# Attention scores in three pairs of PSUM banks, one bank shared by the sums from squares and the projections, and lists of chosen tokens spread by TensorE

## The chip, the cores and the metric

The kernel runs on one core of a Trainium2 chip. The metric is the device time of one execution in microseconds (us). The engines are called as the profile calls them: PE (TensorE, matrix products), PEld (its weight loads), DVE (VectorE), ACT (ScalarE), POOL (GpSimd) and SP (SyncE, which issues most of the DMAs); SPq is SP's instruction queue. PE writes its results to PSUM, which has eight banks of 2 KB a partition; a bank holds 512 float32 numbers a partition.

## The reference, cut to what matters

The program is a chain of four layers on 8 images of 56 x 56 tokens (S = 3136) with 128 channels: a deformable convolution, a whitening of the channels, an attention layer with a mixture of experts (L2), and a linear attention with a second mixture of experts (L3). The change touches the last two.

```python
# L2: attention with keys = queries = values, 8 heads of 16
h = (_ln(t) @ W_k.T).reshape(B, S, 8, 16).transpose(0, 2, 1, 3)
attn = softmax(einsum('bhqd,bhkd->bhqk', h, h) / 4)
t = t + (einsum('bhqk,bhkd->bhqd', attn, h) as tokens) @ W_o.T
# both FFNs: every one of 64 experts takes its best 8 tokens of an image
probs = softmax(_ln(t) @ gate_w.T + gate_b, axis=1)          # over the tokens
topv, topi = top_k(probs over the tokens, 8)                 # [B, 8, 64]
pooled = einsum('bked,bke->bed', _ln(t) gathered at topi, topv)
out = expert_e(pooled)          # two layers, 128 -> 512 -> 128, own weights for each e
t = t + zeros.at[topi].add(out * topv)                       # scattered back
```

The scores are symmetric, since keys and queries are the same: exp(score) of block (b, a) is the transpose of that of block (a, b).

## The kernel before

**Attention (`attend`).** The 3136 tokens of an image are cut into 25 tiles of 128 (`KT`) and 8 query blocks (`NQ`) of three tiles (384 tokens, `KB` = 3); the last block has 448. The work goes through 16 units, one for each image and group of four heads. In a unit each block b, from the last to the first, is multiplied with its own tiles and with those of about half of the other blocks (`stage`): 25 steps for the last block, 13 for each of the others, 116 a unit, 1856 in all. One step is one key tile against one query block, for four heads:

- `scores` (L1168): four matmuls on PE, one for each head on its 32 rows, into four PSUM banks; then ACT takes the exponential, heads 0 and 1 in one instruction over the two banks of the tile `p_s2` (L1175), heads 2 and 3 singly (L1177, tiles `p_s`).
- `weigh` (L1220): `av` collects exp x values over the steps of a block, in one bank.
- `transpose_squares` (L1186), where the tile lies off the block's diagonal: DVE transposes the exponentials in 32 x 32 squares into `sq`, two instructions a step.
- After three such steps (one tile block) `move_squares` has SP issue twelve DMAs (L1202) that put the 32-row squares in their places in `x`, and POOL copies the four on the diagonal (L1213, two a step). This is a job; there are 448.
- `from_squares`: at least `AGE` = 5 steps after its job was made, `avx` (L1220) weighs `x` for the mirrored block, in three steps of a job, into one bank; after the third `take` adds it to the block's sum `acc` on DVE (L1239).

So 1344 steps have a part of an `avx`, 512 have none. The order of the instructions on every engine is the order in which this loop writes them (`manual_schedule`, L1094). On PE a step is: the scores of the next step, a piece of `finish` if there is one, `av`, `avx`.

**`finish` and `choose`.** When the five contributions of a block are in, the generator `finish` divides and, for the second head group of an image, projects, adds the residual, normalises and computes the gate's logits `pr`. It is cut by `yield` into pieces, and the loop does one piece in every second step (`i % 2`); its matmuls (`p_av`, `p_tr`, `p_o`, `p_tr`, `p_g`) use a bank of their own, pool `psm`. When all eight blocks of an image are there, `choose` (L1567 and on) finds the eight best tokens for each expert on DVE (`best`, `at`), their softmax weights (ACT, `every`), writes tokens and weights `found` [64 experts, 2, 8] to DRAM (`route`, L1596, SP) and reads them back as `rw` [128, 2, 4] (`load_choices`, L1628, SP), one chosen token in each partition and column; four gathers by POOL (L1633) and a matmul with the expert pattern (`p_pool`, L1619) make `pooled`.

PSUM in this stage: `ps2` one tile of two banks, `pss` three of one, `psa` (`av`), `psx` (`avx`) and `psm` (pieces) one each: eight banks.

**After the attention.** `run_experts` runs the 64 experts in 16 groups of four, four groups' weights loaded ahead on SP's queue (L1734, L1737); between groups it advances `Spread.prepare` of the images, which reads each list again (`rw`, and `every`, the 512 tokens on all partitions, L1657), gathers the chosen tokens and builds a 512 x 512 matrix that adds up the weights of tokens chosen by several experts (L1674 on DVE, L1678 on POOL). `Spread.run` scatters the result (L1702). Then come the sums of the linear attention's context, `linear_layer` with `choose` once an image, and `run_experts` again for L3.

Of the kernel before, what the change touches and what calls it, by code (L numbers as in the profile page):

```python
# [46 lines left out]
TOP = 8  # L47
# [1021 lines left out]
def attend(tc, k, w, low, tok, kT_in, va_in, t_out, gate_w, gate_b, routes, pooled):  # L1069
# [11 lines left out]
    with ExitStack() as ctx:  # L1081
# [5 lines left out]
        xp = ctx.enter_context(tc.tile_pool(name="atx", bufs=3))  # L1087
        pss = ctx.enter_context(tc.tile_pool(name="ats", bufs=3, space=PSUM))
        ps2 = ctx.enter_context(tc.tile_pool(name="at2", bufs=1, space=PSUM))
        psa = ctx.enter_context(tc.tile_pool(name="ata", bufs=1, space=PSUM))  # L1090
        psx = ctx.enter_context(tc.tile_pool(name="atp", bufs=1, space=PSUM))
# [67 lines left out]
        def scores(u, b, a, i, m):  # L1159

            kT, q, width = keys[u, a][0], queries[u, b], blocks[b][1]
            e = ep.tile([128, 4, QB + 64], F32, name="e")
            s2 = ps2.tile([128, 2, 512], F32, name="p_s2")
            ss = [s2[:, 0], s2[:, 1]]
            ss += [pss.tile([128, 512], F32, tag="s", name="p_s") for _ in range(2)]
            for j in range(4):
                rows = slice(32 * j, 32 * j + 32)
                nc.tensor.matmul(  # L1168
                    ss[j][:m, :width],
                    kT[rows, 128 * i : 128 * i + m],  # L1170
                    q[rows, :width],
                    start=True,
                    stop=True,
                )
            nc.scalar.activation(e[:m, :2, :width], s2[:m, :, :width], AF.Exp)  # L1175
            for j in (2, 3):
                nc.scalar.activation(e[:m, j, :width], ss[j][:m, :width], AF.Exp)  # L1177
            exps[u, b, a, i] = e
# [43 lines left out]
        def from_squares():  # L1222
            u, b, a, x, i, _ = jobs[0]
            assert not (i == 0 and len(jobs) == 1 and moves)
            if i == 0:
                sums[0] = psx.tile([128, QB], F32, tag="x", name="avx")
            e = [x[:, :, (KB * j + i) * 32 : (KB * j + i) * 32 + 32] for j in range(4)]
            weigh(sums[0], u, b, i, 128, e, i == 0, i == KB - 1)
            jobs[0][4] += 1
            if i == KB - 1:  # L1230
                jobs.pop(0)
                take(u, a, sums[0])

        def take(u, b, av):

            width = blocks[b][1]
            to = by_square(acc[b])
            if done[b]:
                nc.vector.tensor_tensor(to, to, in_order(av), ALU.add)  # L1239
            else:  # L1240
                nc.vector.tensor_copy(to, in_order(av))
                if width > QB:
                    nc.vector.tensor_copy(acc[b][:, QB:], av[:, QB:width])
            done[b] += 1
            if done[b] == (1 if b == last else 5):
                work = finish(*parts[u], b)
                urgent.append(work)
                later.append(work)

        def finish(n, g, b):  # L1250

# [22 lines left out]
            yield  # L1274
            if g == 0:
                return
            yield
# [12 lines left out]
            yield  # L1290
# [20 lines left out]
            yield  # L1311
            yield
# [10 lines left out]
            yield  # L1323
# [5 lines left out]
            yield  # L1329
# [5 lines left out]
            yield  # L1335
            ready.append(n)
            if ready.count(n) == NQ:
                yield from choose(nc, k, wp, psm, pr, t_out[n], routes[n], pooled[:, n])
# [21 lines left out]
        av = None  # L1360
        for i, (u, b, a, c, m) in enumerate(steps):
            if i + 1 < len(steps):
                scores(*steps[i + 1])
            if a < NQ and a != b:
                transpose_squares(u, b, a, c)
            keep_squares()
            if i % 2 and urgent:
                work = urgent.pop(0)
                if next(work, later) is later:
                    later.remove(work)  # L1370
            elif i % 2:
                advance(later)
# [29 lines left out]
        while urgent:  # L1402
            work = urgent.pop(0)
            if next(work, later) is later:
                later.remove(work)
        while later:
            advance(later)


def attend_any(tc, k, w, yv, kT_in, va_in, t_out, gate_w, gate_b, routes, pooled, t_g):  # L1410
# [26 lines left out]
    with ExitStack() as ctx:  # L1437
# [3 lines left out]
        for n in range(n_b):  # L1441
# [11 lines left out]
            for _ in choose(nc, k, wp, ps, pr, t_out[n], routes[n], pooled[:, n]):  # L1453
                pass
# [109 lines left out]
def choose(nc, k, wp, ps, pr, t_in, route, pooled):  # L1564
# [30 lines left out]
    with nc.allow_non_contiguous_dma(reason="512 choices"):  # L1595
        nc.sync.dma_start(route.rearrange("x j e -> e x j"), found)  # L1596
    rw = load_choices(nc, wp, route)
    for _ in range(4):
        yield
    rows = wp.tile([128, NC], I32, name="rows")  # L1600
    nc.vector.tensor_copy(rows, rw[:, 0])
# [11 lines left out]
    yield  # L1613
    nc.vector.tensor_tensor(rs, rs, rw[:, 1], ALU.mult)
# [6 lines left out]


def load_choices(nc, pool, route):


    rw = pool.tile([128, 2, NC], F32, name="rw")
    with nc.allow_non_contiguous_dma(reason="512 choices"):
        nc.sync.dma_start(rw, route.rearrange("x (c j) e -> (j e) x c", j=TOP // NC))  # L1628
    return rw
# [11 lines left out]
class Spread:  # L1641
# [3 lines left out]
    def __init__(self, tc, pool, n_b):  # L1645
# [3 lines left out]
        self.rows = pool.tile([128, n_b, NC], I32, name="s_r")  # L1649

    def prepare(self, tc, n, wp, route, t_in, first):
# [3 lines left out]
        rw = load_choices(nc, wp, route)  # L1655
        every = wp.tile([128, TOP * E], F32, name="every")
        nc.sync.dma_start(  # L1657
            every, route[0].rearrange("j e -> (j e)").partition_broadcast(128)
        )
        yield  # L1660
        rows = wp.tile([128, NC], I32, name="rows")
        nc.vector.tensor_copy(rows, rw[:, 0])
        for c in range(NC):
            gather(nc, self.x[:, n, c], t_in, rows[:, c : c + 1])
        if first:
            nc.vector.tensor_scalar(rw[:, 0], rw[:, 0], float(first), None, ALU.add)
        nc.vector.tensor_copy(self.rows[:, n], rw[:, 0])
        if first:
            nc.vector.tensor_scalar(rw[:, 0], rw[:, 0], -float(first), None, ALU.add)
        for c in range(NC):  # L1670
            out = self.weights[:, n]
            if c:
                out = wp.tile([128, TOP * E], F32, name="same")
            nc.vector.tensor_scalar(  # L1674
                out, every, rw[:, 0, c : c + 1], rw[:, 1, c : c + 1], ALU.is_equal, ALU.mult
# [298 lines left out]
def linear_layer(tc, k, w, low, cw, t_in, xT_in, t_out, out, gate_w, gate_b, routes, pooled):  # L1974
# [5 lines left out]
    with ExitStack() as ctx:  # L1980
# [5 lines left out]
        def group(n, g):  # L1986
# [72 lines left out]
            if g == NG - 1:  # L2059
                yield from choose(nc, k, wp, ps, pr, t_out[n], routes[n], pooled[:, n])  # L2060
# [30 lines left out]
def token_layers(tc, k, a, y, out):  # L2091
# [3 lines left out]
    with ExitStack() as ctx:  # L2095
# [9 lines left out]
        routes = [  # L2105
            [dp.tile([2, TOP, E], F32, name=f"route{i}_{n}") for n in range(n_b)]
            for i in range(2)
        ]
# [32 lines left out]
        dest = (t_a, *gates[0], routes[0], pooled[0])  # L2141
# [5 lines left out]
        with tc.tile_pool(name="ex2", bufs=AHEAD) as xp:  # L2147
            ex = Experts(tc, xp, a["L2_ffn_weight1"], a["L2_ffn_weight2"], AHEAD)
            run_experts(tc, k, ex, pooled[0], oe_d[0], routes[0], t_a, [0] * n_b, t_a)
# [4 lines left out]
        with tc.tile_pool(name="ex3", bufs=AHEAD) as xp:  # L2154
            ex = Experts(tc, xp, a["L3_ffn_weight1"], a["L3_ffn_weight2"], AHEAD)
            cw = context_weights(tc, k, w, mp, tot, den)
            dest = (cw, t_a, xT_d, t_c, out, *gates[1], routes[1], pooled[1])
# [3 lines left out]
            with both.Else():  # L2161
# [4 lines left out]
                tc, k, ex, pooled[1], oe_d[1], routes[1], t_c, firsts, [flat] * n_b  # L2166
# [3 lines left out]
def run_experts(tc, k, ex, pooled, oe, routes, t_in, firsts, dests):  # L2170


    with ExitStack() as ctx:
# [3 lines left out]
        todo = [  # L2177
            spread.prepare(tc, n, wp, routes[n], t_in[n], firsts[n])
            for n in range(len(t_in))
        ]  # L2180
        for _ in ex.run(k, pooled, oe):
            advance(todo, 2)
        while todo:
            advance(todo, 2)
# [57 lines left out]
```

## Time and profile before

| | us |
|---|---|
| median of 3 runs | 8446.42 |
| the runs | 8442.32 to 8447.27 |
| profiled execution | 8463.81 |
| its span, first to last instruction | 8462.0 |
| convolution and whitening, keys | 0 to 2388 |
| attention loop and what is left over after it | 2388 to 7310 |
| L2 experts and scatter | 7310 to 7490 |
| sums of the context | 7490 to 7741 |
| linear layer | 7741 to 8215 |
| L3 experts | 8215 to 8372 |
| last scatter | 8372 to 8462 |

In a timeline a line gives the start and the time from the first start to the last end of equal neighbouring instructions, then engine, source line, operation, output and inputs, shapes, and in brackets how long the engine had idled before and what ended that. A line of waits gives engine, line and what it waited for, then total, number and the longest. Matmuls overlap, so the distance of starts says more than their durations.

### The profile page before, as it was taken

How to read it: one execution, taken by the hardware profiler on the slowest of the kernel's cores; microseconds unless marked ns; L12 is line 12 of the kernel's file. 1: busy time of each engine (PE TensorE's matmuls, PEld its weight loads, DVE VectorE, ACT ScalarE, POOL GpSimd, SP SyncE). 2: the span in 40 equal slices, each digit the busy share in tenths (PEclk: the TensorE clock that was granted, in tenths of full speed). 3: DMA queues.
4: the chain of work that ended last, by engine and by line, in shares of the span. 5: the costliest groups of instructions: out<-in, count | busy, mean ns of one | idle time of the engine just before them, and what ended most of it. 6: DMA issues, size and time to landing. Idle time of an engine off the chain costs nothing. (4 is left out here: it accounts for less than half of the span.)

```text
span 8462.0 us, 158965 instructions
## 1 busy us (share of the span) xinstructions
PE 6881.1 (81%) x59199; PEld 2885.4 (34%) x59199; DVE 5195.3 (61%) x10405; ACT 4446.5 (53%) x8821; POOL 3375.8 (40%) x2891
## 2 busy tenths in 40 slices
PE   8976777755589998998999989989989999456734
PEld 4544444423323332332332323323323323135522
DVE  4457667515656676676666766766766766346751
ACT  2324555531256666666666666666666666046740
POOL 0003454541234444444444444444444444333653
PEclk6657777777789999999999999999999999589767
DMA  4333323236768777877777877877877777443544
GB/s 99 86 80 65 75 54 77 51 74 190 222 179 194 180 190 175 192 184 177 188 173 186 192 168 186 193 171 180 195 170 183 188 177 175 149 138 108 129 110 141
DMA packets 773029, 1278.98 MB, mean 151 GB/s; under 512 B 160341, under 2 KB 531498, under 8 KB 765226
## 3 DMA queue, kind: packets, MB, share of 16 engines
q1 hardware_dynamic: 762266, 1252.28, 60.9%
q0 software_dynamic: 6144, 12.60, 0.5%
q8 instruction: 478, 7.83, 0.4%
q10 hardware_dynamic: 3824, 3.68, 0.1%
q14 instruction: 317, 2.60, 0.1%
HBM read 290.36 MB, written 185.03 MB: 56 GB/s over the span
## 5 line engine op out<-in xcount | busy, mean ns | idle before, releaser
L1213 POOL COPY x<-sq 32x1152 f32<-32x1152 f32 x1792 | 2048.0, 1143 | 2320.7 <-issue 1164.7
L1186 DVE STREAM_TRANSPOSE sq<-e 128x768 f32<-128x768 f32 x2688 | 2446.7, 952 | 780.2 <-ACT e L1175 337.0
L1175 ACT ACTIVATE e<-p_s 128x768 f32<-128x768 f32 (+2 forms) x1856 | 1546.6, 833 | 1741.4 <-PE p_s L1168 1647.4
L1168 PE MATMUL p_s<-q,kT 32*128 32x384 f32 (+2 forms) x14848 | 1946.9, 550 | 101.4 <-DVE q L1154 27.0
L1220 PE MATMUL av<-e,va 128*32 128x384 f32 (+2 forms) x14848 | 1648.4, 516 | 14.3 <-DVE acc L1239 14.3
L1177 ACT ACTIVATE e<-p_s 128x384 f32<-128x384 f32 (+2 forms) x3712 | 1650.4, 501 | 0.1
L1220 PE MATMUL avx<-x,va 128*32 128x384 f32 x10752 | 1144.1, 498 | 169.8 <-DMA x<-sq 112.5
L1168 PEld LDWEIGHTS p_s<-q,kT 32*128 32x128 f32 (+1 forms) x14848 | 693.5, 181 | 1365.8 <-ACT e L1177 793.4
L1220 PEld LDWEIGHTS av<-e,va 128*32 128x32 f32 (+1 forms) x14848 | 293.4, 108 | 970.1 <-issue 896.5
L1220 PEld LDWEIGHTS avx<-x,va 128*32 128x32 f32 x10752 | 335.4, 111 | 791.7 <-issue 751.9
L1239 DVE TENSOR_TENSOR acc<-acc,avx 128x384 f32<-128x384 f32 x336 | 186.3, 554 | 342.5 <-PE avx L1220 341.3
L554 PE MATMUL p_f<-x1T,w 128*128 128x448 f32 x448 | 229.9, 634 | 99.9 <-ACT y L510 47.1
L116 PE MATMUL p_tr<-ident,xn 112*128 112x112 f32 x672 | 134.3, 339 | 189.3 <-DVE xn L107 145.6
L507 POOL TENSOR_TENSOR rs<-rs,mhalf 112x4 f32<-112x4 f32 x112 | 120.3, 1074 | 379.8 <-DVE rs L506 359.0
L504 DVE BATCH_NORM_STATS2 st<-p_tok 112x6 f32<-112x128 f32 x448 | 116.4, 277 | 250.8 <-PE p_tok L536 250.6
L1055 POOL TENSOR_TENSOR rs<-rs,mhalf 112x4 f32<-112x4 f32 (+2 forms) x136 | 168.5, 1239 | 253.2 <-DVE ntop L1853 126.8
L424 PE MATMUL p_w<-ident,wide 112*88 112x112 f32 x896 | 179.6, 362 | 105.3 <-ACT wT L426 38.5
L559 PE MATMUL p_f<-hid,w 128*128 128x448 f32 x448 | 213.9, 624 | 42.2 <-ACT hid L555 27.3
L366 POOL MEMSET wide<- 112x10416 f32 x1 | 8.8, 8779 | 584.6 <-DMA om_d<-om 584.6
L264 DVE SCALAR_TENSOR_TENSOR acc<-xp,dw,acc 128x3136 f32<-128x3136 f32 x64 | 223.0, 3485 | 2.3
L1901 ACT ACTIVATE xn<-t,ms,rs 112x128 f32<-112x128 f32 x448 | 185.3, 488 | 74.3 <-DVE ms L1894 74.3
L1308 POOL TENSOR_TENSOR rs<-rs,mhalf 128x3 f32<-128x3 f32 (+1 forms) x72 | 58.9, 820 | 400.8 <-DVE rs L1307 394.2
(337 smaller groups left out, 8562.4 us busy)
## 6 DMA issues: line engine op xcount, KB each, us to landing
x<-sq SPq DMA_DIRECT2D x5376, 144.0 KB
w<-in_L_ffn_weight_dram SPq DMA_DIRECT2D x64, 1024.0 KB
px<-strips SPq DMA_DIRECT2D x64, 616.0 KB
va_d<-va SPq DMA_DIRECT2D x16, 1600.0 KB
kT_d<-kT SPq DMA_DIRECT2D x16, 1568.0 KB
t<-t_a SPq DMA_DIRECT2D x16, 1568.0 KB
kT<-kT_d SPq DMA_DIRECT2D x112, 192.0 KB
va<-va_d SPq DMA_DIRECT2D x112, 192.0 KB
```

Source lines behind the costliest of these rows:

```text
L264: nc.vector.scalar_tensor_tensor(acc, view, dw[:, j : j + 1], acc, ALU.mult, ALU.add)
L424: nc.tensor.transpose(p[:, g], around[:, :, g], k.ident[:T, :T])
L554: nc.tensor.matmul(p, q.w1[:, f * 128 : (f + 1) * 128], x1T, start=True, stop=True)
L559: nc.tensor.matmul(p, q.w2[:, f], hid[:, f], start=(f == 0), stop=(f == 3))
L1168: nc.tensor.matmul(ss[j][:m, :width], kT[rows, 128 * i : 128 * i + m], q[rows, :width], start=True, stop=True,)
L1175: nc.scalar.activation(e[:m, :2, :width], s2[:m, :, :width], AF.Exp)
L1177: nc.scalar.activation(e[:m, j, :width], ss[j][:m, :width], AF.Exp)
L1186: nc.vector.transpose(sq[:, :, i, j : j + 2].rearrange("p s j c -> p j s c"), exps[u, b, a, i][:, j : j + 2, :QB].rearrange("p j (s c) -> ...
L1213: nc.gpsimd.tensor_copy(*moves.pop(0))
L1220: nc.tensor.matmul(out, keys[u, b][1][:m, i, j, :], e[j], start=start, stop=stop)
L1239: nc.vector.tensor_tensor(to, to, in_order(av), ALU.add)
L1901: nc.scalar.activation(out[:, i], x[:, i], AF.Identity, bias=ms[:, i : i + 1], scale=rs[:, i : i + 1])
```

## The change

Three things change.

1. In `attend` the scores go to `pss`, three tiles of two banks (six banks), so that each step has two tiles and two exponentials over two banks each. `ps2` and `psx` are gone; `avx` takes the one bank of `psm` that the pieces of `finish` and `choose` use.
2. A piece says by its `yield` whether the next one needs that bank (`True`). A piece that needs it only goes on when no job is part way (`free`), and `later` pieces at most every second step (`turn`).
3. The lists stay in SBUF, in `choices` [128, image, 2, 4]. `choose` spreads `found` over 128 partitions with two matmuls by the identity (`p_take`) in place of the write and read through DRAM. `Spread.prepare` no longer reads lists: it multiplies the identity by the tokens (`own`) and adds up over the partitions with a matmul by ones, which puts all 512 tokens on every partition (`every`, in PSUM).

```diff
@@ attend
         pss = ctx.enter_context(tc.tile_pool(name="ats", bufs=3, space=PSUM))
-        ps2 = ctx.enter_context(tc.tile_pool(name="at2", bufs=1, space=PSUM))
         psa = ctx.enter_context(tc.tile_pool(name="ata", bufs=1, space=PSUM))
-        psx = ctx.enter_context(tc.tile_pool(name="atp", bufs=1, space=PSUM))
         psm = ctx.enter_context(tc.tile_pool(name="atm", bufs=1, space=PSUM))
@@ scores
-            s2 = ps2.tile([128, 2, 512], F32, name="p_s2")
-            ss = [s2[:, 0], s2[:, 1]]
-            ss += [pss.tile([128, 512], F32, tag="s", name="p_s") for _ in range(2)]
+            ss = [pss.tile([128, 2, 512], F32, name="p_s") for _ in range(2)]
...
-            nc.scalar.activation(e[:m, :2, :width], s2[:m, :, :width], AF.Exp)
-            for j in (2, 3):
-                nc.scalar.activation(e[:m, j, :width], ss[j][:m, :width], AF.Exp)
+            for j in range(2):
+                nc.scalar.activation(
+                    e[:m, 2 * j : 2 * j + 2, :width], ss[j][:m, :, :width], AF.Exp
+                )
@@ from_squares
-                sums[0] = psx.tile([128, QB], F32, tag="x", name="avx")
+                sums[0] = psm.tile([128, QB], F32, tag="m", name="avx")
@@ finish: each yield now says whether the next piece needs psm
-            yield
+            yield False   # or True
@@ attend, the loop
+        def go_on(work):
+            try:
+                work[1] = next(work[0])
+            except StopIteration:
+                later.remove(work)
...
-            if i % 2 and urgent:
-                work = urgent.pop(0)
-                if next(work, later) is later:
-                    later.remove(work)
-            elif i % 2:
-                advance(later)
+            free = not jobs or jobs[0][4] == 0
+            if urgent and free:
+                go_on(urgent.pop(0))
+            elif later and i > turn + 1 and (free or not later[0][1]):
+                go_on(later[0])
+                turn = i
@@ choose
-        nc.sync.dma_start(route.rearrange("x j e -> e x j"), found)
-    rw = load_choices(nc, wp, route)
-    for _ in range(4):
-        yield
+    yield True
+    p = ps.tile([128, 2, NC], F32, tag="m", name="p_take")
+    for j in range(TOP // NC):
+        nc.tensor.matmul(
+            p[E * j : E * j + E],
+            k.ident[:E, :E],
+            found[:, :, j :: TOP // NC],
+            start=True,
+            stop=True,
+        )
     rows = wp.tile([128, NC], I32, name="rows")
-    nc.vector.tensor_copy(rows, rw[:, 0])
+    nc.vector.tensor_copy(rows, p[:, 0])
+    nc.vector.tensor_copy(taken, p)
@@ Spread.prepare
-        rw = load_choices(nc, wp, route)
-        every = wp.tile([128, TOP * E], F32, name="every")
-        nc.sync.dma_start(
-            every, route[0].rearrange("j e -> (j e)").partition_broadcast(128)
-        )
-        yield
         rows = wp.tile([128, NC], I32, name="rows")
-        nc.vector.tensor_copy(rows, rw[:, 0])
+        nc.vector.tensor_copy(rows, taken[:, 0])
         for c in range(NC):
             gather(nc, self.x[:, n, c], t_in, rows[:, c : c + 1])
...
+        own = wp.tile([128, NC, 128], F32, name="own")
+        nc.vector.tensor_tensor(
+            own,
+            k.ident.unsqueeze(1).to_broadcast([128, NC, 128]),
+            taken[:, 0].unsqueeze(2).to_broadcast([128, NC, 128]),
+            ALU.mult,
+        )
+        yield
+        every = ps.tile([128, TOP * E], F32, name="every")
+        nc.tensor.matmul(
+            every, self.ones, own.rearrange("p c q -> p (c q)"), start=True, stop=True
+        )
```

More of the change, by code (lines that the diff above doesn't have):

```diff
@@ L1066, in query_blocks, with attend @@
     ]
-def attend(tc, k, w, low, tok, kT_in, va_in, t_out, gate_w, gate_b, routes, pooled):
+def attend(tc, k, w, low, tok, kT_in, va_in, t_out, gate_w, gate_b, taken, pooled):
     nc = tc.nc
@@ L1168, in scores @@
                 nc.tensor.matmul(
-                    ss[j][:m, :width],
+                    ss[j // 2][:m, j % 2, :width],
                     kT[rows, 128 * i : 128 * i + m],
@@ L1245, in take @@
             if done[b] == (1 if b == last else 5):
-                work = finish(*parts[u], b)
+                work = [finish(*parts[u], b), True]
                 urgent.append(work)
@@ L1289, in finish @@
             nc.vector.tensor_copy(aT[:, :width], p[:, :width])
-            yield
+            yield True
             p = psm.tile([128, KB + 1, C], F32, tag="m", name="p_o")
@@ L1310, in finish @@
                 )
-            yield
-            yield
+            yield False
+            yield False
             xn = wp.tile([128, KB + 1, C], F32, name="xn")
@@ L1322, in finish @@
                 )
-            yield
+            yield True
             xT = wp.tile([C, QB + 64], F32, name="xT")
@@ L1328, in finish @@
             nc.vector.tensor_copy(xT[:, :width], p[:, :width])
-            yield
+            yield True
             p = psm.tile([E, 512], F32, tag="m", name="p_g")
@@ L1334, in finish @@
             )
-            yield
+            yield False
             ready.append(n)
             if ready.count(n) == NQ:
-                yield from choose(nc, k, wp, psm, pr, t_out[n], routes[n], pooled[:, n])
+                yield from choose(nc, k, wp, psm, pr, t_out[n], taken[:, n], pooled[:, n])
+        def go_on(work):
[3 more added lines that the diff above has]
+                later.remove(work)
         ready = []
@@ L1359, in attend @@
         scores(*steps[0])
-        av = None
+        av, turn = None, -2
         for i, (u, b, a, c, m) in enumerate(steps):
@@ L1401, in attend, with attend_any @@
             from_squares()
[L1402 to L1405, printed above, removed]
+        for work in urgent:
+            go_on(work)
         while later:
-            advance(later)
-def attend_any(tc, k, w, yv, kT_in, va_in, t_out, gate_w, gate_b, routes, pooled, t_g):
+            go_on(later[0])
+def attend_any(tc, k, w, yv, kT_in, va_in, t_out, gate_w, gate_b, taken, pooled, t_g):
     nc = tc.nc
@@ L1452, in attend_any @@
                 nc.vector.tensor_scalar(pr[:, cols], p, gate_b, None, ALU.add)
-            for _ in choose(nc, k, wp, ps, pr, t_out[n], routes[n], pooled[:, n]):
+            for _ in choose(nc, k, wp, ps, pr, t_out[n], taken[:, n], pooled[:, n]):
                 pass
@@ L1561, in attention_any, with choose @@
             divide(nc, k, wp, psm, av_sb, att, g, c)
-def choose(nc, k, wp, ps, pr, t_in, route, pooled):
+def choose(nc, k, wp, ps, pr, t_in, taken, pooled):
     best = wp.tile([E, TOP], F32, name="best")
@@ L1594, in choose @@
     nc.vector.tensor_scalar(found[:, 1], found[:, 1], tot, None, ALU.mult)
-    with nc.allow_non_contiguous_dma(reason="512 choices"):
-        nc.sync.dma_start(route.rearrange("x j e -> e x j"), found)
-    rw = load_choices(nc, wp, route)
-    for _ in range(4):
-        yield
+    yield True
+    p = ps.tile([128, 2, NC], F32, tag="m", name="p_take")
[7 more added lines that the diff above has]
+        )
     rows = wp.tile([128, NC], I32, name="rows")
-    nc.vector.tensor_copy(rows, rw[:, 0])
+    nc.vector.tensor_copy(rows, p[:, 0])
+    nc.vector.tensor_copy(taken, p)
     x = wp.tile([128, NC, C], F32, name="chosen")
@@ L1612, in choose @@
     rs = rsqrt(nc, k, wp, mv, NC)
-    yield
-    nc.vector.tensor_tensor(rs, rs, rw[:, 1], ALU.mult)
+    yield True
+    nc.vector.tensor_tensor(rs, rs, taken[:, 1], ALU.mult)
     for c in range(NC):
@@ L1620, in choose @@
     nc.vector.tensor_copy(pooled, p)
[L1623 to L1629, printed above, removed]
 def gather(nc, out, table, rows):
@@ L1649, in __init__, with prepare @@
         self.rows = pool.tile([128, n_b, NC], I32, name="s_r")
-    def prepare(self, tc, n, wp, route, t_in, first):
+        self.ones = pool.tile([128, 128], F32, name="s_1")
+        tc.nc.vector.memset(self.ones, 1.0)
+    def prepare(self, tc, k, n, wp, ps, taken, t_in, first):
         nc = tc.nc
-        rw = load_choices(nc, wp, route)
-        every = wp.tile([128, TOP * E], F32, name="every")
-        nc.sync.dma_start(
-            every, route[0].rearrange("j e -> (j e)").partition_broadcast(128)
+        rows = wp.tile([128, NC], I32, name="rows")
+        nc.vector.tensor_copy(rows, taken[:, 0])
+        for c in range(NC):
+            gather(nc, self.x[:, n, c], t_in, rows[:, c : c + 1])
+        nc.vector.tensor_scalar(self.rows[:, n], taken[:, 0], float(first), None, ALU.add)
+        own = wp.tile([128, NC, 128], F32, name="own")
[4 more added lines that the diff above has]
+            ALU.mult,
         )
         yield
-        rows = wp.tile([128, NC], I32, name="rows")
-        nc.vector.tensor_copy(rows, rw[:, 0])
[L1663 to L1669, printed above, removed]
+        every = ps.tile([128, TOP * E], F32, name="every")
+        nc.tensor.matmul(
+            every, self.ones, own.rearrange("p c q -> p (c q)"), start=True, stop=True
+        )
         for c in range(NC):
@@ L1674, in prepare @@
             nc.vector.tensor_scalar(
-                out, every, rw[:, 0, c : c + 1], rw[:, 1, c : c + 1], ALU.is_equal, ALU.mult
+                out,
+                every,
+                taken[:, 0, c : c + 1],
+                taken[:, 1, c : c + 1],
+                ALU.is_equal,
+                ALU.mult,
             )
@@ L1971, in query_bound, with linear_layer @@
         nc.vector.tensor_scalar(small, low[:1], -SMALL3, None, ALU.is_ge)
-def linear_layer(tc, k, w, low, cw, t_in, xT_in, t_out, out, gate_w, gate_b, routes, pooled):
+def linear_layer(tc, k, w, low, cw, t_in, xT_in, t_out, out, gate_w, gate_b, taken, pooled):
     nc = tc.nc
@@ L2059, in group @@
             if g == NG - 1:
-                yield from choose(nc, k, wp, ps, pr, t_out[n], routes[n], pooled[:, n])
+                yield from choose(nc, k, wp, ps, pr, t_out[n], taken[:, n], pooled[:, n])
         pipeline([group(n, g) for n in range(n_b) for g in range(NG)], 1)
@@ L2104, in token_layers @@
         xT_d = dp.tile([n_b, C, S], F32, name="xT_d")
[L2105 to L2108, printed above, removed]
+        choices = [cp.tile([128, n_b, 2, NC], F32, name=f"choices{i}") for i in range(2)]
         oe_d = [dp.tile([n_b, E, C], F32, name=f"oe_d{i}") for i in range(2)]
@@ L2140, in token_layers @@
         query_bound(tc, k, w, a["L3_attn_w_in"], low3, small3)
-        dest = (t_a, *gates[0], routes[0], pooled[0])
+        dest = (t_a, *gates[0], choices[0], pooled[0])
         taken = nc.values_load(small[0:1, 0:1], min_val=0, max_val=1)
@@ L2148, in token_layers @@
             ex = Experts(tc, xp, a["L2_ffn_weight1"], a["L2_ffn_weight2"], AHEAD)
-            run_experts(tc, k, ex, pooled[0], oe_d[0], routes[0], t_a, [0] * n_b, t_a)
+            run_experts(tc, k, ex, pooled[0], oe_d[0], choices[0], t_a, [0] * n_b, t_a)
         mp = ctx.enter_context(tc.tile_pool(name="tlm", bufs=1))
@@ L2156, in token_layers @@
             cw = context_weights(tc, k, w, mp, tot, den)
-            dest = (cw, t_a, xT_d, t_c, out, *gates[1], routes[1], pooled[1])
+            dest = (cw, t_a, xT_d, t_c, out, *gates[1], choices[1], pooled[1])
             taken = nc.values_load(small3[0:1, 0:1], min_val=0, max_val=1)
@@ L2165, in token_layers, with run_experts @@
             run_experts(
-                tc, k, ex, pooled[1], oe_d[1], routes[1], t_c, firsts, [flat] * n_b
+                tc, k, ex, pooled[1], oe_d[1], choices[1], t_c, firsts, [flat] * n_b
             )
-def run_experts(tc, k, ex, pooled, oe, routes, t_in, firsts, dests):
+def run_experts(tc, k, ex, pooled, oe, taken, t_in, firsts, dests):
     with ExitStack() as ctx:
@@ L2176, in run_experts @@
         spread = Spread(tc, sp, len(t_in))
[L2177 to L2184, printed above, removed]
+        with tc.tile_pool(name="rxp", bufs=2, space=PSUM) as ps:
+            todo = [
+                spread.prepare(tc, k, n, wp, ps, taken[:, n], t_in[n], firsts[n])
+                for n in range(len(t_in))
+            ]
+            for _ in ex.run(k, pooled, oe):
+                advance(todo, 2)
+            while todo:
+                advance(todo, 2)
         spread.run(tc, oe, lambda n: dests[n][:, :])
```

## The prediction

> **What bounds the kernel now.** I read the page first (busy time by engine, then the costliest groups), then the busy times by stage, then the timeline of a few steady steps of the attention loop, then the waits of PE and of SP's queue in that loop, and last the stretches around the lists of chosen tokens.
>
> ```profile
> PE 6881.1 (81%) x59199; PEld 2885.4 (34%) x59199; DVE 5195.3 (61%) x10405; ACT 4446.5 (53%) x8821; POOL 3375.8 (40%) x2891
> ...
> 2388.00:7197.00 4809.00, 4523.37 (x41754) 1465.43 (x41754) 3223.73 (x4737) 3039.71 (x5674) 2136.32 (x1894) 0.98 0.77 182
> ```
>
> The first line is the page's (busy time, share, instructions), the second the table by stage (start and end, length, busy time of PE, PEld, DVE, ACT and POOL, granted clock, share of DMA, GB/s). It is the attention loop: 57% of the span, PE busy 4523 of 4809 us at a granted clock of 0.98, DVE, ACT and POOL far below. So PE's order sets the pace, and the loop can gain only what PE loses there: idle time, and matmuls that stand in the queue half issued. Two neighbouring steps show the latter:
>
> ```profile
> 3062.39 0.93 PE L1168 MATMUL p_s<-q,kT 32*128 32x384 f32 x8
> ...
> 3064.68 0.93 PE L1168 MATMUL p_s<-q,kT 32*128 32x384 f32 x8
> ...
> 3065.53 0.85 PE L1220 MATMUL av<-e,va 128*32 128x384 f32 x8
> 3065.64 0.81 ACT L1175 ACTIVATE e<-p_s 128x768 f32<-128x768 f32 x1 [0.71 <-PE p_s L1168]
> 3066.34 0.87 ACT L1177 ACTIVATE e<-p_s 128x384 f32<-128x384 f32 x2
> 3066.50 0.67 PEld L1168 LDWEIGHTS p_s<-q,kT 32*128 32x128 f32 x8 [0.81 <-ACT e L1175]
> 3066.50 1.29 PE L1168 MATMUL p_s<-q,kT 32*128 32x384 f32 x8
> ```
>
> From 3062.39 to 3064.68 a step with `avx` takes 2.29 us, all of it PE work (scores .86 to `av`, `av` .67, `avx` .76, by the distances of their starts). The next step has no `avx`: scores .86 and `av` .78 would be 1.64, but the next scores only start 1.82 later, when the double exponential (ended 3066.45) has emptied the one two-bank tile. They then take 1.29 in place of .93, since their fourth matmul needs the bank of the exponential for j=2. So a step without `avx` costs .18 + .36 = .54 us more than its work. By the loop's code 512 of 1856 steps have none.
>
> **The change part by part.** The sum is made against the profiled execution (8463.8; span 8462.0), which lies 17.4 over the median of the runs, 8446.4.
>
> 1. *Score banks.* Three tiles of two banks in place of one of two and three of one; PE's matmuls stay, ACT has two 768-wide exponentials (2 x .81) for .81 + .87, so ACT's own work falls from 1.68 to 1.62 a step and stays just under PE's 1.64. Scores now start at once; their second pair needs the pair that the step before filled first, which its exponential leaves 1.83 after that step's start: .19 late after a bare 1.64 step. The step after starts `av` when both exponentials are done (.96 + 1.62 = 2.58 after the scores' start, against 1.64 + .86 = 2.50): the same lateness, not another. So .19 is left of .54. Before, 82 pieces of the division and the projections (`finish`) lay on steps without `avx` and filled the gap; (512 - 82) x .54 = 232, of which I leave 80 (.19 on 280 steps without a piece is 53, and half as much again for late exponentials): -150. Bounds: 0 if something else binds (rival 1), -232.
>
> 2. *One bank for `avx` and the pieces.* Pieces go on only when no job is part way, so by following the loop's code 233 land on steps without `avx`, 141 (with those of `choose`) share a step with the first `avx` of a job. There `avx` waits until DVE has read the piece out: .56 to .85 for the copy, of which `av` (.67) covers most if DVE is idle; with two transposes (.95 each) ahead of the copy, up to 1.9 more. Between 0 and 1.9 I take .45 each, nearer the idle end, as DVE is 67% busy here: +63. A piece that follows a job's third `avx` waits for the addition (.55) instead; behind scores (.86) that is hidden where DVE is free, and
>
> ```profile
> DVE acc L1239 <- PE avx L1220: 330.7, 333, 2.4
> PE avx L1220 <- DMA x<-sq: 112.5, 36, 13.2
> ```
>
> says it was waiting for `avx` in 333 of 448 cases: about 115 late ones, a third of them with a piece, 1 us each: +35. Together +98 (bounds 0 to +331: every one of the 141 at 1.9, every one of the 115 at .55). The pieces' work on PE (.48 to .86 each) is unchanged.
>
> 3. *No write and read of the lists through DRAM in the loop.* The queue of SP, around one image's list:
>
> ```profile
> 3209.38 7.53 SPq L1202 DMA_DIRECT2D x<-sq  x12
> 3221.76 0.67 SPq L1596 DMA_DIRECT2D route<-found  x1
> 3232.08 0.39 SPq L1628 DMA_DIRECT2D rw<-route  x1
> 3232.56 17.01 SPq L1202 DMA_DIRECT2D x<-sq  x24
> ```
>
> The read `rw` waits 10 us for the write to land, and the next job's twelve transfers stand behind it. PE pays: seven of the 36 waits above, one for each list written in the loop, are 11.2 to 13.4 us, 82 in all. They go: -82. POOL's gathers waited on the same read with the copies of `x` behind them: -15. What replaces it: two 64-row matmuls and two small DVE copies, 1 us an image, in part 2's 141.
>
> 4. *What the faster steps meet.* A job's twelve issues take 7.53, landing 2.1 more after the last: 9.6 from the transposes to its first `avx`, five steps later. With two steps without `avx` among them, five steps are 3 x 2.28 + 2 x 1.64 = 10.1, less some .4 between transposes and `avx`. That leaves .1 where there was 1.1; with one, .8. I give back +30 for jobs whose issues are slowed by loads (bounds 0 to +160, rival 1).
>
> Loop: -150 + 98 - 82 - 15 + 30 = -119.
>
> 5. *After the loop.* The last list:
>
> ```profile
> 7280.75 0.17 DVE L1601 CAST rows<-rw 128x4 int32<-128x4 f32 x1 [13.19 <-DMA rw<-route]
> ```
>
> 13.2 us for the way through DRAM, against some 1.3 for the matmuls (DVE waits 1.29 for the four small ones of `p_pool` nearby): -12, nothing covers it. One more piece (`p_g`, .79 and its .61 addition) stays after the loop: +2. Loads of lists no longer stand on SP ahead of the experts' weights: -4.
>
> 6. *Linear layer.* SP waits 66 us in eight places for these writes; prefetched tiles cover most of it: -10 (0 to -40).
>
> 7. *End of the linear layer and last experts* (timelines of SP, DVE and PE).
>
> ```profile
> 8195.27 0.38 SPq L1628 DMA_DIRECT2D rw<-route  x1
> 8196.14 0.37 SPq L1734 DMA_DIRECT2D w<-in_L_ffn_weight_dram  x1
> ...
> 8199.53 0.17 DVE L1601 CAST rows<-rw 128x4 int32<-128x4 f32 x1 [12.40 <-DMA rw<-route]
> ...
> 8245.50 2.34 DVE L1753 COPY x<-pooled 128x512 f32<-128x512 f32 x1
> ...
> 8247.99 1.93 PE L1766 MATMUL p_h<-w,x 128*32 128x512 f32 x8 [33.40 <-DVE x L1753]
> ```
>
> Two lists go through DRAM one after the other, six of eight weight loads stand behind the second, and the copy `x` stands on DVE behind pieces of `prepare` that wait for POOL, so PE idles 33 us. After: `pooled` some 17 earlier, weights already loading; but `x` still stands behind the gathers of two images (10 us of POOL), and `prepare` gains a 128x512 multiply (.6) and a matmul (1.1) an image, beside idle engines. I take -31 (0 to -45); the experts then run at the pace of their weights (PE busy 94 of the stage's 157 us, 8215 to 8372), so the shift lasts. The final chain of scatters is unchanged.
>
> Sum: -119 - 14 - 10 - 31 = **-174**: 8290 against the profiled execution, **8272** against the median.
>
> **A rule against it.** The trace of before shows `avx` alone in its bank, waited for by one reader. The Trainium skill ("PSUM — Partial Sum Buffer", section "PSUM bank collisions raise a hardware error") says that the compiler's scheduler puts a dependency between any two engines' instructions on one bank and quadrant, reads too. No run here shows its price; part 2 has it as a term, rival 2 takes it at its upper bound.
>
> **The rivals.**
> - *Rival 1, SP binds* (.2): twelve issues take longer than 7.5 (the row above has 24 in 17.0, 8.5 a job), first `avx`s wait for landing, and the gain of part 1 comes back: 448 x .36 = +160 in place of +30, total -44: 8402. For it: the slack of part 4 and DMA busy 0.77. Against: only 36 waits on `x` before, few of them long.
> - *Rival 2, the shared bank* (.16, slower): first `avx` and pieces stand behind DVE's transposes nearly each time. It decides from 272 in place of 98, 1.06 us on each of the 141 + 115 places; at its upper bound of 331 the time is 8505. For it: DVE has two transposes in every step without `avx`, 1.9 us in a step that shrinks to 1.64 to 1.83. Against: the 333 cases of an idle DVE.
> - *Rival 3, a free bank* (.14): DVE is idle at nearly each piece and the scores gain all: -232 and +20 in parts 1 and 2 would be 8112; half way there, 8190.
> - *The lists change nothing* (.04): another load takes the place of `rw` on SP; of the sum, parts 1, 2, 4 and 6 and the small ends of 5 stay: -34, 8412.
>
> **How the numbers follow.** The forecast case has .46, its own range is 8210 to 8340. The 8-in-10 range leaves out rival 2 and the lowest part of rival 3: 8165 to 8430. A measurement can tell about 0.2% (17 us) from no change, so same is 8429 to 8463: a fifth of rival 1 and half of the last case, .06. Faster: .46 + .16 + .14 + .02 = .78. Slower: rival 2, .16.
>
> **What would show it.** Right: scores of 0.93 to 1.12 us after steps without `avx`, distance of such steps 1.64 to 1.85; no wait of `avx` over 5 us on `x`; the loop's stretch about 4690; `x<-pooled` near 8071, some 54 after the last MAX8 of the linear layer (85 before). Wrong: a wait of `avx` on DVE's readout of over 150 us in all (rival 2), or of `avx` on `x` over 150 (rival 1); PE idle before the last experts still over 30 us.

## The result and the profile after

The changed kernel takes 8229.2 us in the median (8220.02 to 8243.62) against 8446.85 before: ratio 0.9745, 95% interval 0.9728 to 0.9762, or 218 us less. The prediction was 8272 (174 less), its range 8165 to 8430. The sign, and most of the size, came as forecast; the parts of the sum did not, as the runs below show.

Marks in the two profiled executions (spans 8462.0 and 8220.0) place the difference:

| stage (first mark to last mark) | before | after | change | forecast |
|---|---|---|---|---|
| start to the loop's first scores | 2388.3 | 2378.4 | -10 | 0 |
| attention loop, first to last scores | 4792.6 | 4609.4 | -183 | -119 |
| last scores to the eighth `pooled` | 111.2 | 102.3 | -9 | -10 |
| that `pooled` to the first `p_h` | 16.5 | 9.9 | -7 | -4 |
| first `p_h` to the end of the L2 scatter | 181.9 | 188.7 | +7 | 0 |
| end of that scatter to the last MAX8 of the linear layer | 670.5 | 674.2 | +4 | -10 |
| last MAX8 to the copy `x<-pooled` | 84.5 | 40.7 | -44 | -31 |
| from there to the end of the last scatter | 208.5 | 208.4 | 0 | 0 |

The rows add up to -242 (the 8.0 us behind the last scatter are the same in both). The first ten us lie in stages that the change does not touch, and the profiled executions stand 17 us above and 7 us below their medians, so the 218 of the medians and these 242 agree.

The page of the changed kernel, two of its costliest groups (line, engine, operation | busy, mean ns | idle before), and from its table by stage the loop (start and end, length, busy time of PE, PEld, DVE, ACT and POOL, granted clock, share of DMA, GB/s):

```profile
PE 6738.0 (82%) x59295; PEld 2807.8 (34%) x59295; DVE 5171.3 (63%) x10425; ACT 4329.0 (53%) x6965; POOL 3372.7 (41%) x2891
...
L1174 ACT ACTIVATE e<-p_s 128x768 f32<-128x768 f32 (+2 forms) x3712 | 2887.7, 830 | 1675.3 <-PE p_s L1166 1455.8
...
L1166 PE MATMUL p_s<-q,kT 32*128 32x384 f32 (+2 forms) x14848 | 1828.4, 547 | 32.6 <-DVE q L1154 21.0
```

```profile
2378.00:6988.00 4610.00, 4375.98 (x41712) 1379.67 (x41712) 3184.94 (x4738) 2920.94 (x3816) 2130.24 (x1890) 0.99 0.79 190
```

PE still sets the pace. The scores' busy time fell from 1946.9 to 1828.4 with the same 14848 instructions: fewer matmuls stand half issued, and fewer run at half the clock (below). The timeline shows the step that the prediction worked out:

```profile
2480.64 0.93 PE L1166 MATMUL p_s<-q,kT 32*128 32x384 f32 x8
2481.50 0.85 PE L1219 MATMUL av<-e,va 128*32 128x384 f32 x8
2482.28 1.10 PE L1166 MATMUL p_s<-q,kT 32*128 32x384 f32 x8
```

A step without `avx` and without a piece now lasts 1.64 (2480.64 to 2482.28; 1.82 before), and the scores after it 1.10 instead of 1.29. By the traces 284 steps of the changed kernel are like this, 427 of the kernel before. Waits of the changed kernel in its loop (engine, line and what it waited for: total, times, longest), and below them the one of the kernel before that answers to the last:

```profile
DVE acc L1238 <- PE avx L1219: 304.2, 321, 2.5
...
ACT e L1174 <- DVE sq L1185: 165.1, 152, 3.0
...
PE avx L1219 <- DMA x<-sq: 75.1, 56, 5.0
```

```profile
ACT e L1175 <- DVE sq L1186: 69.8, 50, 4.9
```

The seven waits of `avx` of 11 to 13 us are gone (the longest is 5.0), but there are 56 where there were 36, and ACT's exponentials wait for DVE's transposes three times as often.

A long wait costs PE more than its length. The kernel before, behind the first of those seven waits, and a row of a table of windows (its columns as above) for this stretch:

```profile
3243.80 1.51 PE L1220 MATMUL avx<-x,va 128*32 128x384 f32 x8 [13.21 <-DMA x<-sq]
3245.24 1.66 PE L1168 MATMUL p_s<-q,kT 32*128 32x384 f32 x8
3246.84 1.51 PE L1220 MATMUL av<-e,va 128*32 128x384 f32 x8
3248.12 1.34 PE L1220 MATMUL avx<-x,va 128*32 128x384 f32 x8
3249.39 0.93 PE L1168 MATMUL p_s<-q,kT 32*128 32x384 f32 x8
```

```profile
3237.00:3249.00 12.00, 5.20 (x32) 1.34 (x32) 1.10 (x2) 1.57 (x3) 0.00 (x0) 0.50 0.97 226
```

The granted clock is 0.50 there. The four groups take 5.59 us (3243.80 to 3249.39) where their usual distances add up to 3.05, so 2.5 us more are lost. Each of the seven waits has such a stretch, which ends 3.0 to 6.2 us after the wait. By the clock records of the traces, the loop before has 226 us at half clock, with PE busy in 159 of them, the changed one 100 and 88. Half of the busy time, 80 and 44 us, is an estimate of the loss: some 36 of the loop's 183 us. The prediction has no such term.

After the loop, DVE's timeline at the last list, and those of SP, DVE and PE before the last experts:

```profile
7077.92 0.22 DVE L1598 TENSOR_SCALAR found<-found,tot 64x8 f32<-64x8 f32 x1
7078.63 0.16 DVE L1610 CAST rows<-p_take 128x4 int32<-128x4 f32 x1 [0.49 <-PE p_take L1602]
```

```profile
7961.54 2.48 SPq L1749 DMA_DIRECT2D w<-in_L_ffn_weight_dram  x1
```

```profile
8003.55 0.17 DVE L1659 CAST rows<-choices 128x4 int32<-128x4 f32 x1 [4.77 <-DMA s_x<-t_c,rows]
8003.63 0.59 DVE L1765 COPY x<-pooled 128x512 f32<-128x512 f32 x1
```

```profile
8004.27 1.93 PE L1778 MATMUL p_h<-w,x 128*32 128x512 f32 x8 [10.45 <-DVE x L1765]
```

The list takes 0.49 us of waiting instead of 13.19. The last of the eight first loads of weights is issued 43 us before the experts start, and PE's wait for `x` is 10.45 instead of 33.40; what is left of it is the gathers of two images (`s_x<-t_c`), as forecast.

### The profile page after: what moved, and what is told of

It reads as the page before. It is cut to its first block, busy times and chain, and to the rows that moved or that the text cites. A ratio compares the mean times of both kernels' runs of the same rounds, so it can differ in the third digit from the quotient of the medians.

```text
span 8220.0 us, 157423 instructions
## 1 busy us (share of the span) xinstructions
PE 6738.0 (82%) x59295; PEld 2807.8 (34%) x59295; DVE 5171.3 (63%) x10425; ACT 4329.0 (53%) x6965; POOL 3372.7 (41%) x2891
## 5 line engine op out<-in xcount | busy, mean ns | idle before, releaser
L1174 ACT ACTIVATE e<-p_s 128x768 f32<-128x768 f32 (+2 forms) x3712 | 2887.7, 830 | 1675.3 <-PE p_s L1166 1455.8
L1166 PE MATMUL p_s<-q,kT 32*128 32x384 f32 (+2 forms) x14848 | 1828.4, 547 | 32.6 <-DVE q L1154 21.0
L1166 PEld LDWEIGHTS p_s<-q,kT 32*128 32x128 f32 (+1 forms) x14848 | 617.1, 180 | 1229.2 <-issue 931.8
L250 ACT COPY pj<-p_in 56x512 f32<-56x512 f32 x112 | 64.9, 579 | 267.5 <-PE p_in L243 248.6
```

What stands on the lines that cost most here:

```text
L1166: nc.tensor.matmul(ss[j // 2][:m, j % 2, :width], kT[rows, 128 * i : 128 * i + m], q[rows, :width], start=True, stop=True,)
L1174: nc.scalar.activation(e[:m, 2 * j : 2 * j + 2, :width], ss[j][:m, :, :width], AF.Exp)
```

## The experiments

Three figures are taken from each kernel's one trace besides its time. *Loop* is the distance from the first to the last scores. *First avx* is the sum over the jobs up to the last scores of (start of the first `avx` matmul - start of `av` in that step - .67, or .78 in the wide block), so PE's wait there whatever its cause. *Late scores* is the sum over the steps of (start of the last of the eight score matmuls - start of the first - .447, or .52 in the wide block) where that is positive, so in the main matmuls held by a full bank. Both sums also hold what these instructions lose at half clock. The profiled executions lie up to 17 us off their medians, so smaller differences between loops tell nothing. Ratios are against the kernel before as it ran beside each of them.

| kernel | median us | ratio (95%) | loop | first avx | late scores |
|---|---|---|---|---|---|
| before | 8446.85 | 1 | 4792 | 197 | 167 |
| E1 lists only | 8306.28 | 0.9817 (0.9793 to 0.9841) | 4689 | 121 | 166 |
| E3 order only | 8360.99 | 0.9887 (0.9860 to 0.9913) | 4679 | 149 | 130 |
| E4 order and shared bank | 8415.84 | 0.9943 (0.9921 to 0.9964) | 4746 | 186 | 130 |
| E2 order, shared bank, pairs | 8389.71 | 0.9910 (0.9884 to 0.9936) | 4721 | 258 | 82 |
| changed kernel (all four) | 8229.20 | 0.9745 (0.9728 to 0.9762) | 4609 | 214 | 61 |
| E7 lists and order | 8237.75 | 0.9754 (0.9718 to 0.9790) | 4604 | 101 | 127 |
| E9 lists, order, pairs, own bank | 8209.78 | 0.9715 (0.9688 to 0.9743) | 4616 | 155 | 122 |
| E6 as E9, pieces only in steps with an `avx` | 8329.80 | 0.9863 (0.9828 to 0.9899) | 4718 | 181 | 149 |
| E11 before, AGE 6 | 8352.05 | 0.9875 (0.9852 to 0.9898) | 4673 | 91 | 164 |
| E5 changed kernel, AGE 6 | 8188.43 | 0.9702 (0.9665 to 0.9738) | 4548 | 144 | 82 |
| E8 as E7, AGE 6 | 8127.77 | 0.9632 (0.9596 to 0.9668) | 4497 | 7 | 126 |
| E10 as E9, AGE 6 | 8077.89 | 0.9540 (0.9516 to 0.9564) | 4449 | 6 | 131 |
| E12 as E10, third buffer for e | 8071.86 | 0.9543 (0.9513 to 0.9572) | 4446 | 8 | 119 |

**E1 to E4: one part at a time.** The kernel before took 8459.2 beside these four. E1 has the loop of before and the new `choose` and `prepare`:

> Before with the lists kept in SBUF alone: PSUM, scores and the order of the pieces in the attention loop as before. My theory (the parts of the sum stand side by side): the seven waits of 11 to 13 us on x go and POOL's gathers come earlier, so the loop's 4792 us become about 4695; after the loop 49 us go as between the two traces: 8300 in all. Rival, the lists cost the loop nothing once anything else changes there (the wait moves to another transfer on SP): only what lies after the loop goes, 8398.

E1 measured 8306 (-153), its loop 4689: the lists are worth 103 us in the loop and about 50 after it, as the theory had it. No wait of `avx` on `x` is longer than 2.6 us there, and 92 us of its loop are at half clock instead of 226.

E2 has the changed loop and the old `choose` and `prepare`:

> The attention loop of the changed kernel (three pairs of banks, avx and pieces in one bank, the new order of pieces), but the lists go through DRAM as before. My theory: the loop goes from 4792 to about 4706 (what the whole change gave there, 183, less 97 for the lists), nothing after it: 8361. Rival 1 (the landing of x takes the gain of the score banks back): 8420 or more. If the banks alone made the change: 8280 or less.

8390 (-70), between the theory and rival 1; the loop is 4721. E3 keeps the old banks and only lets the pieces go on between jobs:

```diff
-            if i % 2 and urgent:
+            free = not jobs or jobs[0][4] == 0
+            if urgent and free:
...
-            elif i % 2:
-                advance(later)
+            elif later and i > turn + 1 and (free or not later[0][1]):
+                go_on(later[0])
+                turn = i
```

> Before with the new order of the pieces of finish and choose alone (they go on only between jobs), banks and lists as before. By the traces a piece makes a step without avx .40 us longer and a step with avx .3 to .58, so moving 150 pieces gives about -15: 8432. If the order is the source of the gain in the loop, 8380 or less.

8361 (-98). My expectation of -15 fell: the order alone gives as much in the loop (-113) as the lists. E4 adds one edit, the shared bank:

```diff
-                sums[0] = psx.tile([128, QB], F32, tag="x", name="avx")
+                sums[0] = psm.tile([128, QB], F32, tag="m", name="avx")
```

> As the run with the new order alone, and avx moved into the bank of the pieces; scores keep their old banks, lists go through DRAM. The difference to that run is the price of sharing the bank. My prediction's term: +98, so 8530. The changed kernel's trace shows 52 us more between av and the first avx in steps with a piece, which would give 8485 to 8500. Rival: sharing costs nothing, 8432.

8416, 55 above E3 (loop +67): sharing costs, though less than 98. From E4 to E2 only the pairs come in, and the time falls by 26. The last two columns say why so little: late scores fall by 48, and the first `avx` waits 72 more. The waits from 2388 to 6800 us of E4 and then of E2:

```profile
PE avx L1221 <- DMA x<-sq: 80.1, 37, 10.3
```

```profile
PE avx L1219 <- DMA x<-sq: 114.0, 65, 10.8
```

PE reaches the first `avx` of a job sooner and meets `x` still on its way, 65 times instead of 37. That is rival 1's mechanism, at about half its size.

**E5 to E8: the waits at the first avx.** E5 gives the data one step more, and changes nothing else:

```diff
-AGE = 5
+AGE = 6
```

> The changed kernel with AGE = 6: a job's first avx comes one step (about 2.1 us) later, nothing else. In the changed kernel's loop PE waits 214 us between av and the first avx, 136 of it in steps without a piece. Theory (twelve issues and their landing are late, rival 1 of the prediction): most of the 136 goes, ratio to before 0.958 to 0.965, where the changed kernel has 0.9745. Rival (these waits are for the shared bank or for DVE, which a later avx does not change): 0.972 to 0.977.

0.9702, short of the theory's range and beyond the rival's; the loop lost 61. In steps without a piece the first `avx` waits 5 us instead of 136, so late landing was there. In steps with a piece the wait rose from 78 to 139, so the shared bank was there too. Most of that rise is not a wait that was hidden before: the later jobs put 79 of the `p_av` pieces ahead of a first `avx`, where the changed kernel has 31, and `avx` waits 1.1 us behind each. E6 takes the pieces' PSUM tiles from the pairs, leaves `avx` a bank of its own, and lets pieces go on only where the next job is old enough for its `avx` (the comments are not in the kernel):

```diff
-        psm = ctx.enter_context(tc.tile_pool(name="atm", bufs=1, space=PSUM))
+        psx = ctx.enter_context(tc.tile_pool(name="atm", bufs=1, space=PSUM))   # avx
+        psm = Pairs()    # .tile() gives the first bank of a pss pair
...
-            free = not jobs or jobs[0][4] == 0
+            free = not jobs or i - jobs[0][5] >= AGE
...
-            elif later and i > turn + 1 and (free or not later[0][1]):
+            elif later and i > turn + 1 and free:
```

> The changed kernel, but the pieces of finish and choose take one pair of the three for scores, avx has its bank for itself, and pieces go on in steps that have a part of an avx. The price of sharing by the runs with old score banks was 55 to 68 us. Theory: it goes, and the score banks' gain stays: 8229 - 60 in the first chip's time, ratio about 0.968. Rival (pieces in steps with avx delay DVE's transposes and so the next jobs, as in the kernel before): the gain is lost again, 0.972 or more.

0.9863: the rival's side, and 100 us worse than the changed kernel. Its order is not that of before: by the trace all of its 374 pieces with matmuls stand in steps with an `avx`, where the kernel before has 279 of 368 and the changed kernel 141 of 373. As the edit moved two things, E9 below takes them apart. E7 undoes the two PSUM edits:

> The changed kernel with the score banks and the bank of avx of before: lists in SBUF and the new order of pieces, without shared bank and pairs. If the parts add as the single runs say (lists -153, order -98, on 8459), 8208, ratio 0.970, which is below the changed kernel's 0.9745: shared bank and pairs together cost about 30 us. If pairs pay once the lists are out of the way: 0.977 or more.

0.9754, between the two readings, so the parts do not add. Lists and order overlap: the seven waits that the lists remove are 83 us in the kernel before and 62 in E3. Shared bank and pairs together neither gain nor cost at AGE = 5 (loops 4604 and 4609). E8 is E7 with AGE = 6:

> As the run before it with AGE = 6. Theory (late landing): the first avx's waits, about 100 us there, go to below 40, ratio 0.960 to 0.964; the waits for score banks (240 us with the old banks) stay or grow, since PE now meets them first. Rival: no change against AGE = 5.

0.9632; the first `avx` waits 7 us in all. The old banks are not in the way of that: late scores stay at 126.

**E9 to E12: own bank against shared bank, with and without the landing.** E9 is E6 with the changed kernel's order:

> The changed kernel with its own order of pieces, but avx has its bank for itself and the pieces take one pair of the three for scores. It differs from the run with pieces in the steps with avx in the order alone, and from the changed kernel in the bank of the pieces alone. If sharing the bank is what makes the first avx wait (214 us in the changed kernel, 101 with old banks and an own bank): ratio to before 0.965 to 0.969. If pairs speed the scores and the landing of x then takes it back, whatever the bank: 0.972 to 0.977, the first avx's waits still over 170 us.

0.9715, between the two readings. Against E6 the order alone is worth 102 us of the loop; part of that is the clock, as PE is busy at half clock for 217 us in E6 and for 119 here. Against the changed kernel the own bank brings nothing in the loop (4616 to 4609): the first `avx` waits 59 less, and the scores, whose pairs the pieces now take, are 61 later. E10 removes the landing:

> As the run before it with AGE = 6, so that neither the bank nor the landing stands before the first avx. Theory: first avx's waits under 20 us, scores keep what the pairs give (48 us before the scores and 61 in them, against 107 and 130 with the old banks): ratio 0.955 to 0.960, below the 0.9632 of the old score banks with AGE = 6. Rival: the pieces in pairs hold the scores up by what the pairs give, 0.963 or more.

0.9540, better than expected, and the fastest of these with E12. Its loop is 98 us shorter than E5's, which differs in the bank of the pieces alone, and 48 shorter than E8's, which differs in the score banks and in the bank of the pieces. Waits of `avx` on `x` in E5 and then in E10, from 2388 to 6800 us:

```profile
PE avx L1219 <- DMA x<-sq: 27.8, 27, 1.7
```

```profile
PE avx L1233 <- DMA x<-sq: 1.6, 3, 0.8
```

> The kernel before with AGE = 6 alone. Its first avx waits 197 us in the loop, 82 of it for the lists through DRAM. Theory: landing is late by itself, the step more takes 60 to 100 of them: ratio 0.988 to 0.993. Rival (late landing appears only once the loop is faster): 0.995 or more.

E11, 0.9875: landing was late before the change too. First `avx` fell by 106, to 91, of which the seven waits for the lists still hold 65 (10.5 the longest); up to 6800 us the trace has no other wait of `avx` on `x`. AGE also moves the pieces: 126 stand in steps without `avx`, 89 before. E12 asks whether the new wait of ACT on DVE (165 us in the changed kernel) reaches the end:

> As the run with pairs, an own bank for avx and AGE = 6, with a third buffer for the exponentials e (the pool ate, 3 in place of 2). There ACT's exponentials wait 117 us in 88 places for DVE to have transposed the e of two steps before; in the changed kernel it is 161 us in 147, in the kernel before 67 in 47. If those waits reach PE through the scores' banks, they go and the loop loses 30 to 60 us: ratio 0.947 to 0.951. Rival: scores and av are held up by the pieces in the pairs and the work of ACT alone, 0.953 to 0.956.

From E12's waits in the loop:

```profile
ACT e L1188 <- DVE sq L1199: 2.6, 1, 2.6
```

The wait is gone (117 in E10), the time is not (0.9543 against 0.9540; 30 to 60 us were expected if it reached the end): it cost nothing that can be told.

## Why the prediction was right, and where it was wrong

1. *Score banks, -150.* The mechanism was right nearly to the hundredth: bare steps of 1.64, scores behind them .17 late (median of 77 like steps; forecast .19, before .36). The sum was mis-attributed. It priced all the gaps of .54 in steps without `avx` as the banks' gain, while the new order alone fills many of them. By the traces 232 such steps hold a piece instead of 89: 143 x .54 = 77, which is the order's. A piece there is nearly free with the old banks: in E3 a like step lasts 2.12 with a piece, the scores behind it .07 late, and without one 1.82 and .36 (medians). With that order in place the pairs gave 26 (E4 to E2), and 48 of the loop where neither bank nor landing held the first `avx` (E8 to E10). This step of the prediction failed: it took the removal of one wait and the filling of it as one term, and gave the order none.
2. *The order*, a term that was missing. E3 gives 113 us of the loop, and E9 against E6, whose order is another, 102. Late scores account for 37 of E3's and the first `avx` for 48; scores that start earlier give 143 x .18 = 26.
3. *Shared bank, +98.* At AGE = 5 it measured +67 in the loop with old banks (E4 - E3). With pairs nothing can be told at AGE = 5, since what the own bank brings is lost again where the pieces hold a score pair (E9). At AGE = 6 it is 98, net of that loss (E5 - E10). The size was of the right order, its working was not. The +35 rests on a misread row. The 333 waits are those of the additions at L1239, of which there are 336; the 112 first contributions are copies at L1241 with a row of their own:

```profile
DVE acc L1241 <- PE avx L1220: 118.5, 91, 3.8
```

So 24 of 448 were late, not 115, and by the prediction's own rule that part is +8 and the term +71. The rule of the Trainium skill ("PSUM — Partial Sum Buffer", section "PSUM bank collisions raise a hardware error": two engines' accesses to one bank and quadrant are put one after the other) speaks against the change as cited. The runs agree in direction: in steps with a piece the first `avx` waits 139 us in E5 and 1 in E10. They do not tell that rule from the plain reuse of the one tile in that bank. Rival 2 did not decide, since its 272 us were never near.
4. *Lists, -82 and -15 in the loop.* E1's loop is 103 shorter, its first `avx` waits 76 less. The sum was right, its split is not shown: behind the seven waits the half clock cost an estimated 18 us (half of the 35 us from their ends to the clock's return), which the prediction did not have, and no run shows 15 for POOL's gathers.
5. *What the faster steps meet, +30.* The pairs alone raised the first `avx`'s wait by 72 (E4 to E2). Rival 1 was a part of the outcome rather than a case of its own; the term was less than half of what it should have been. Landing was also late before the change, with its longer steps (E11), which the slack of 1.1 us in the prediction does not have.
6. *After the loop, -14, -10, -31.* Measured -16, +4 and -44. In the linear layer SP's 66 us of waits for lists went and gave nothing; SP's waits for `p_q` there rose from 85 to 209 us. Before the last experts the loads issued 43 us ahead and the copy `x` gave more than reckoned. Not forecast: +7 in the L2 experts, where PE now runs `every` between the experts' matmuls and waits for DVE's `own`, 7.93 us in one place.

So the total came out 44 us short with two terms too large (pairs, shared bank), two missing (order, clock) and one too small (landing); their errors partly cancel, and that part of the agreement is luck. What was not luck is the lists: alone they give 153 of the 218 us (E1), and they were read mostly from one kind of wait.

In E10 late scores are still 131, about those of the old banks. Its trace says why: 62 us of them come behind the 233 steps with a piece and no `avx`, and 3 us in E5, which differs in the bank of the pieces alone. So the pieces in the pairs hold them.

Two things stay open. Why the order brings the first `avx` 48 us earlier (E3) is shown in part: 21 of them lie at the seven waits for lists (83 to 62). Pieces bring DVE work with them, and in which steps it delays the transposes of a job was not tried by itself. And what halves the clock is not shown beyond its place around the long waits; no run changed it alone.

## What to carry to other kernels

When an in-order engine has gaps, count once what fills them: here moving independent pieces of work into the gaps was worth 98 us, and removing the wait that made them then gave 26 (48 of the loop once nothing else held the step). Before speeding up the steps of a pipeline, check the slack of the transfers that are timed in steps; a distance of five steps was already short before the change, and one more step (AGE = 6) alone gave 104 us, more than the new PSUM layout. A DMA round trip of a small list is paid above all by what stands behind its wait on the issuing queue: seven lists made PE wait 83 us for other transfers.

## What the runs showed of the hardware that was not expected

One step more between a job's issue and its use is worth 1.2% to the kernel before (E11) and 1.2 to 1.8% to kernels with lists and order (E7 to E8, E9 to E10), although the wait that the trace names, `avx` on `x`, is only 42 us (E7) to 97 (before) from 2388 to 6800 us. The first-`avx` sums, which do not ask for the cause, carry most of it: 106 of the 119 us that the loop loses in E11, 94 of 107 in E8, 149 of 167 in E10. Behind waits of 11 to 13 us PE ran at half the clock for another 3.0 to 6.2 us. ACT waiting 117 us for DVE's transposes cost nothing that can be told (E12), at 66% busy in ACT and 74% in DVE (E10). The list of 512 choices took 13.19 us by way of DRAM and 0.49 us of waiting by way of PE and PSUM.
